# Two states in one scan tile: a selective scan in layer 1 regrouped as 64 channels x 2 states

## Chip, core and metric

The kernel runs on one core of a Trainium2 chip. The metric is the device time of one execution in microseconds (us). The core has five engines with a queue each: TensorE (PE in the profile, PEld for its weight loads), VectorE (DVE), ScalarE (ACT), GpSimd (POOL) and SyncE (SP, which issues most of the DMAs). SBUF is the working memory of 128 partitions, PSUM the memory that TensorE writes its sums to.

## The reference, cut to what matters

The program is a chain of four layers on images of 64 channels and 64 x 64 pixels. Only layer 1 is changed. It scans each image's 4096 pixels in four orders ("ways": by rows, by columns, and both backwards), with 128 channels and 16 states:

```
xs = concatenate([x_hwwh, flip(x_hwwh)], axis=1)        # 4 ways
x_dbl = einsum('bkdl,kcd->bkcl', xs, x_proj_w)
dts, Bs, Cs = split(x_dbl, [DT_RANK, DT_RANK + N], axis=2)
delta = softplus(einsum('bkrl,kdr->bkdl', dts, dt_w) + dt_b)
A = -exp(A_logs)

def step(h, inp):
    u, d, b, c = inp
    dA = exp(d[..., None] * A)
    h = dA * h + d[..., None] * b[:, :, None, :] * u[..., None]
    y = sum(h * c[:, :, None, :], axis=-1)
    return (h, y)
...
out_y = ys + xs * Ds
y = out_y[0] + inv_y[0] + unwh(out_y[1]) + unwh(inv_y[1])
```

So for each image, way, channel and state there is a first-order recurrence along 4096 pixels; its result is multiplied by C and summed over the 16 states, and the four ways are added up. What follows (normalization, gate, projection, feed-forward) is not changed.

## The kernel before

**Units of work.** An image's 4096 pixels are four chunks of T = 1024. One step (class `Step` in `layer1`) is one image b, one way k, one chunk j: 8 x 4 x 4 = 128 steps, in the order of line 1294's list, ways in the order 1, 3, 2, 0. A step has 16 scan tiles, one for each state, of 128 channels by 1024 pixels. `stream` (from line 433) runs through all 2048 tiles in one loop, software-pipelined by hand: the order of the instructions in this loop is the order in each engine's queue.

**One tile i, before.** Loads on SP (line 1239): one row of B and one of C, each broadcast from HBM to 128 partitions (512 KB each). `fetch(i + 5)` and `fetch_c(i + 3)` issue them ahead, into pools of four B tiles and five C tiles. `multiply_b(i + 2)` (line 484): GpSimd makes hb = du * B, into a pool of three. `decay(i + 2)` (line 491): ScalarE makes dA = exp(dt * A) in PSUM, two buffers. `scan(i)` (line 500): VectorE runs the recurrence over dA and hb; the result goes over dA in PSUM, or, for the states in `shared`, to an SBUF tile h. `multiply_c` (line 514): the product with C, on VectorE, or for the shared states 1, 4, 7, 10, 13 on GpSimd. ScalarE keeps the last column for the next chunk (`keep`, line 1249). `gather(i - 2)` calls `mm` (line 306): TensorE adds the product tile to the sum acc in PSUM with an identity matrix as weights; each 128x512 fp32 matmul stands as two passes in the profile, so a tile has four. When the last tile of a step is summed, `drain` (lines 1264 and 1266) moves acc to the image y: ScalarE copies it for the first way, VectorE adds it to y for the three others. `late` and `first` in the loop put a gather behind the background work or behind the scan.

**Preparing a step.** While a step runs, `prepare` makes the next one's data, one piece a tile from tile 2 on: TensorE projects u (x_dbl), ScalarE copies it and sends B and C to HBM, TensorE and ScalarE make dt (softplus), GpSimd makes du = dt * u (line 1236). dt and du are 128 channels by 1024 pixels, in two buffers each.

**Background tasks.** Preparing the images (`begin`), and normalization, output and feed-forward of those that are scanned (`finish`, `feed`), are cut into pieces that `advance` puts between the tiles, at one place in the loop. They use all engines and SP's queue (for instance line 910 loads 64-partition pieces of an image, lines 1133 and 1144 are VectorE's gating products, line 973 spreads a row over 128 partitions). A piece that holds the one PSUM buffer "mm" must be followed by its next ones before others come.

`Choice` is a pool that can be switched to a second one: while no scan runs, or at the end, the background tasks borrow the scan's tiles "dA" and "h".

Of the kernel before, what the change touches and what calls it, by code (L numbers as in the profile page):

```python
# [10 lines left out]
F32 = mybir.dt.float32  # L11
AF = mybir.ActivationFunctionType
ALU = mybir.AluOpType
# [93 lines left out]
def layouts(i):  # L107
# [29 lines left out]
    o["l1_dtb"] = i[p + "dt_b"].T  # L137
    o["l1_A"] = i[p + "A_logs"].reshape(4, 128, NS).transpose(1, 0, 2)
    o["l1_D"] = i[p + "Ds"].reshape(4, 128).T
# [68 lines left out]
def like(ap, ref):  # L208

    if len(ref.shape) == 2:  # L210
        return ap
    return ap.rearrange("p (a b) -> p a b", b=ref.shape[2])
# [38 lines left out]
class Choice:  # L251
# [5 lines left out]
    def tile(self, shape, dtype, name):  # L257
        if self.turns:
            self.second = not self.second
        return self.other.tile(shape, dtype, name=self.name) if self.second else self.pool.tile(shape, dtype, name=name)  # L260


def two(pool):


    return Ring([pool(f"pe{j}", 1, space=PSUM) for j in range(2)])


class Net:
# [313 lines left out]


    def layer0(self, src, dst):

# [272 lines left out]
    def layer1(self, src, dst):  # L859
        nc, tc, d = self.nc, self.tc, self.d  # L860
        mid = self.hbm["x1a"]
        with ExitStack() as ctx:
            pool = lambda n, b, **k: ctx.enter_context(tc.tile_pool(name="l1" + n, bufs=b, **k))
            cp, p1, p2, img, tp = pool("c", 1), pool("p1", 1), pool("p2", 2), pool("img", 2), pool("t", 5)
            pp = pool("pp", 1, space=PSUM)
            bp = pool("b", 4), pool("cc", 5)
            pools = (bp, pool("hb", 3), pool("hc", 3), pool("h", 3), two(pool), pool("pa", 1, space=PSUM))

            pp, tp = Choice(pp, pools[4], "dA"), Choice(tp, pools[3], "h")
            hp, h1 = pool("h3", 3, space=DRAM), pool("h1", 4, space=DRAM)  # L870
# [105 lines left out]
            def begin(b):  # L976
# [3 lines left out]
                ahead = {0: tokens(src, b, 0)}  # L980
                yield False

# [220 lines left out]
            class Step:  # L1203
                start, early, late = 2, 8, True
                shared = (1, 4, 7, 10, 13)
                shaped = staticmethod(lambda t: t)

                def __init__(self, b, k, j):
                    self.b, self.k, self.j, self.c, self.rev = b, k, j, 3 - j if k >= 2 else j, k >= 2
                    self.lanes = [(slice(None), A[:, k, :])]  # L1210

# [4 lines left out]
                def prepare(self):  # L1216
# [14 lines left out]
                    yield CALM  # L1231
                    dt = self.dt = p2.tile([128, T], F32, name="dt")
                    net.softplus_act(dt, pt, dtb[:, k : k + 1])
                    yield False
                    du = self.du = p2.tile([128, T], F32, name="du")
                    nc.gpsimd.tensor_tensor(like(du, u), like(dt, u), u, ALU.mult)

                def load(self, n, m, t):
                    nc.sync.dma_start(t, self.bc[m * NS + n : m * NS + n + 1, :].to_broadcast([128, T]))

# [11 lines left out]

                def skip(self, acc):
                    if self.k == 0:
                        net.mm(acc, skip[:, 0, :], self.u, start=True, stop=False)
                    return self.k == 0

                def drain(self, acc):
                    hold = images[self.b]
                    if self.k == ways[0] and self.j == 0:  # L1260
                        hold["y"] = img.tile([128, L], F32, name="img")
                    y = view(hold["y"], self.k, self.c)
                    if self.k == ways[0]:
                        nc.scalar.copy(y, like(acc, y))
                    else:
                        nc.vector.tensor_tensor(y, like(acc, y), y, ALU.add)  # L1266

# [16 lines left out]
            with tc.manual_schedule():  # L1284
# [9 lines left out]
                steps = [Step(b, k, j) for b in range(NB) for k in ways for j in range(4)]  # L1294
                self.stream(pools, (5, 2, 3), steps, behind, rest)

# [853 lines left out]
```

## Time and profile before

| what | value |
|---|---|
| three runs | 24767.98, 24765.61, 24763.93 us; median 24765.61 |
| profiled execution: span | 24763.3 us; the page lists no other time of its own beside it |
| layer 1's scan loop, first scan to last product | 1216 to 8487 us |
| its steady part, 2000 to 8000 us: VectorE, GpSimd, TensorE, ScalarE busy | 5471.63, 5562.17, 5165.06, 3262.36 us |
| the same: DMA share, GB/s | 0.90, 316 |
| products with B on GpSimd in it (line 484) | 1679 |
| loads of B and of C in it | 1678 and 1678, 512 KB each |
| products with C on VectorE and on GpSimd in it | 1153 and 524 |

How to read it: busy time is the time in which an engine executes, not the time in which it is held by another. A row of a group is: line, engine, operation, output<-inputs, shapes, count, then busy time, mean duration in ns, and the idle time before these instructions with what ended it. A row of waits is: who waited, for whom, us in total, how often, the longest. A row of the timeline is: start, duration (both us), engine, line, operation, tiles. A row of busy time by stretches has the stretch, its length, busy time and count for each engine, the clock granted to TensorE, the DMA share and the GB/s. Durations of neighbours overlap a little, so the distance from start to start is what an instruction costs in a dense queue.

### The profile page before, as it was taken

To read this page: it belongs to the slowest core of one execution; us is meant where nothing else is said; L and a number is where in the kernel's file an instruction comes from. 1 tells how busy PE (TensorE), PEld (TensorE's weight loads), DVE (VectorE), ACT (ScalarE), POOL (GpSimd) and SP (SyncE) were. 2 spreads that over 40 slices of the span, in tenths; PEclk is the share of its full clock that TensorE was granted. 3 is DMA by queue.
4 is the path that set the end of the run, shared out by engine and by line. 5 is a ranking of instruction groups with operands and counts; after the bars stand their busy time and mean duration, and the time that the engine had idled before them with its cause. 6 is when DMAs were issued, how large, how long until landed. Compare 5 with 4: busy or idle time off the path is not lost. (4 is left out here: it accounts for less than half of the span.)

```text
span 24763.3 us, 192937 instructions
## 1 busy us (share of the span) xinstructions
PE 21205.6 (86%) x53146; PEld 8272.3 (33%) x53146; DVE 22452.5 (91%) x12956; ACT 14796.2 (60%) x18824; POOL 22125.0 (89%) x10580
## 2 busy tenths in 40 slices
PE   8877888888888888888888888888888888888888
PEld 6522333333333323322333333333333333333333
DVE  5399999999999779978999999999999999999999
ACT  4355555555555456624666666666666666666666
POOL 0199999999999669977999999999999999999999
PEclk9888999999999999999999999999999999999999
DMA  2399899898998669933555555555555555555554
GB/s 65 93 319 326 308 321 318 310 319 314 313 318 311 238 211 339 343 103 93 168 173 169 173 167 173 168 173 167 173 169 173 168 173 169 173 169 173 169 173 158
DMA packets 1835292, 5282.68 MB, mean 213 GB/s; under 512 B 533712, under 2 KB 539924, under 8 KB 1831904
## 3 DMA queue, kind: packets, MB, share of 16 engines
q1 hardware_dynamic: 1809632, 5207.00, 63.0%
q10 hardware_dynamic: 24576, 63.33, 0.7%
q8 instruction: 423, 6.93, 0.1%
q14 instruction: 661, 5.41, 0.1%
HBM read 5112.85 MB, written 156.11 MB: 213 GB/s over the span
## 5 line engine op out<-in xcount | busy, mean ns | idle before, releaser
L484 POOL TENSOR_TENSOR hb<-du,bc 128x1024 f32<-128x1024 f32 x4608 | 10746.4, 2360 | 204.5 <-DVE h L500 137.9
L306 PE MATMUL acc<-hc,ident 128*128 128x512 f32 x18560 | 8788.0, 614 | 87.6 <-DVE img L1266 49.9
L491 ACT ACTIVATE dA<-dt,w_A 128x512 f32<-128x512 f32 x8192 | 5673.1, 693 | 3923.3 <-DVE hc L514 2873.1
L500 DVE TENSOR_TENSOR_SCAN dA<-dA,hb 128x1024 f32<-128x1024 f32 x3320 | 7580.9, 2283 | 188.4 <-ACT dA L491 101.0
L306 PE MATMUL acc<-h,ident 128*128 128x512 f32 x8064 | 4652.9, 706 | 2430.0 <-POOL h L514 2400.9
L306 PEld LDWEIGHTS acc<-hc,ident 128*128 128x128 f32 x18560 | 3639.8, 200 | 5214.2 <-issue 4562.5
L484 POOL TENSOR_TENSOR hb<-du,b 128x1024 f32<-128x1024 f32 x2048 | 4919.7, 2476 | 467.4 <-DVE dA L500 205.6
L514 DVE TENSOR_TENSOR hc<-dA,bc 128x1024 f32<-128x1024 f32 x3232 | 3956.8, 1224 | 244.4 <-issue 4.5
L491 ACT ACTIVATE dA<-dt,w_l_A 128x1024 f32<-128x1024 f32 x2560 | 2863.6, 1119 | 1004.6 <-DVE hc L514 764.6
L500 DVE TENSOR_TENSOR_SCAN h<-dA,hb 128x1024 f32<-128x1024 f32 x1416 | 3229.1, 2280 | 82.0 <-ACT dA L491 80.2
L306 PEld LDWEIGHTS acc<-h,ident 128*128 128x128 f32 x8064 | 1569.1, 212 | 5155.8 <-POOL h L514 3484.1
L514 POOL TENSOR_TENSOR h<-h,bc 128x1024 f32<-128x1024 f32 x1376 | 3243.1, 2357 | 8.3 <-DVE h L500 8.3
L500 DVE TENSOR_TENSOR_SCAN dA<-dA,carry,hb 128x1024 f32<-128x1024 f32 x1320 | 3094.2, 2344 | 124.9 <-POOL hb L484 57.2
L514 DVE TENSOR_TENSOR hc<-dA,c 128x1024 f32<-128x1024 f32 x1408 | 1723.7, 1224 | 118.3 <-DMA c<-bc 7.2
L514 POOL TENSOR_TENSOR h<-h,c 128x1024 f32<-128x1024 f32 x640 | 1566.4, 2447 | 7.5 <-ACT carry L1249 6.9
L491 ACT ACT_TABLE_LOAD x1128 | 1447.2, 1283 | 19.7
L500 DVE TENSOR_TENSOR_SCAN h<-dA,carry,hb 128x1024 f32<-128x1024 f32 x600 | 1404.6, 2341 | 36.4 <-ACT dA L491 25.2
L1249 ACT COPY carry<-dA 128x1 f32<-128x1 f32 x1056 | 169.4, 160 | 1654.3 <-DVE hc L514 1613.4
L2004 PE MATMUL mm<-xn,taps 128*128 128x512 f32 x2048 | 932.9, 597 | 1.1 <-ACT z L2052 1.1
L721 POOL MEMSET xf<- 128x24 f32 x33 | 4.3, 141 | 851.4 <-PE ps L742 725.2
L2019 PE MATMUL mm<-u,w_xp 128*36 128x512 f32 x1024 | 489.8, 601 | 143.0 <-ACT u L2016 136.3
L2039 POOL TENSOR_TENSOR du<-dt,u 128x1024 f32<-128x1024 f32 x256 | 603.0, 2355 | 9.9 <-ACT dt L415 9.9
(320 smaller groups left out, 18494.0 us busy)
## 6 DMA issues: line engine op xcount, KB each, us to landing
bc<-bc SPq DMA_DIRECT2D x4096, 512.0 KB
b<-bc SPq DMA_DIRECT2D x2048, 512.0 KB
c<-bc SPq DMA_DIRECT2D x2048, 512.0 KB
bc<-bc SPq DMA_DIRECT2D x512, 1024.0 KB
tmp<-rs SPq DMA_DIRECT2D x93, 512.0 KB
raw<-x SPq DMA_DIRECT2D x64, 512.0 KB
inv<-rs SPq DMA_DIRECT2D x64, 512.0 KB
tmp<-x SPq DMA_DIRECT2D x192, 128.0 KB
```

The source lines that it names most:

```text
L306: self.nc.tensor.matmul(o, lhsT, r, start=start, stop=stop)
L484: nc.gpsimd.tensor_tensor(s.shaped(hb[i]), s.shaped(s.du), B.pop(i), ALU.mult)
L491: nc.scalar.activation(dA[i][:, cut], s.dt[:, cut], AF.Exp, scale=A[:, n : n + 1])
L500: nc.vector.tensor_tensor_scan(h[:, way], dA[i][:, way], hb.pop(i)[:, way], s.first(n), ALU.mult, ALU.add)
L514: engine.tensor_tensor(s.shaped(o), s.shaped(h), CC.pop(i), ALU.mult)
L721: nc.gpsimd.memset(x[:, :, HW:], 0.0)
L1249: nc.scalar.copy(self.carry[:, n : n + 1], h[:, last : last + 1])
L2004: nc.tensor.matmul(tokens(px[:, j * W : j * W + W]), w.taps[k][:, m, j * 128 : j * 128 + 128], xn[:, :, f : f + HW], start=m == 0, stop=m ...
L2019: nc.tensor.matmul(pd, w.xp[:, k, j, :], u[:, j * W : j * W + W], start=j == 0, stop=j == 1)
L2039: nc.gpsimd.tensor_tensor(du, dt, u, ALU.mult)
```

## The change

A scan tile now holds 64 channels of two states: partitions 0 to 63 are state 2p, partitions 64 to 127 state 2p + 1; two tiles, one for each half h of the 128 channels, make a pair p. A step still has 16 tiles, in 8 pairs.

- Loads: one B tile and one C tile for a pair, each by two DMAs of 64 partitions (256 KB each), so half the bytes. The pools hold two B and three C tiles.
- dt and du are needed with each half of the channels on both halves of the partitions: `twofold` makes them by four SBUF-to-SBUF DMAs each (256 KB each). dt is now in a single buffer; du is made in place in it once dt is copied.
- B product: one GpSimd instruction for a pair (128 x 2 x 1024, the same B for both halves), into a pool of four pairs.
- The scan of a shared state writes over hb; the product with C always goes into hb, so the pools hc and h are gone. Shared tiles are 1, 4, 7, 10, 13 in even chunks and 1, 4, 6, 9, 12, 14 in odd ones.
- Sums: once for a pair, in four matmuls: for each 512 pixels and each channel half r, 128 rows by 64 columns, weights `ident2[:, :64]` (two identities on top of each other, which add the two states), into the partitions of that half.
- y of the ways before is added into the same sum by an identity matmul at its start, so `drain` is a ScalarE copy for every way.

```diff
+    def stream_pairs(self, pools, steps, behind, rest):
...
+        def fetch(p, m, pool, into):
+            if 2 * p < total:
+                into[p] = pool.tile([128, T], F32, name="bc"[m])
+                steps[2 * p // NS].load(p % (NS // 2), m, into[p])
+
+        def multiply_b(p):
+            if 2 * p < total:
+                s = steps[2 * p // NS]
+                hb[p] = hbp.tile([128, 2, T], F32, name="hb")
+                b = B.pop(p).unsqueeze(1).to_broadcast([128, 2, T])
+                nc.gpsimd.tensor_tensor(hb[p], s.du, b, ALU.mult)
+
+        def decay(i):
+            if i < total:
+                s, h, n = steps[i // NS], i % 2, i % NS // 2
+                dA[i] = pe.tile([128, T], F32, name="dA")
+                nc.scalar.activation(dA[i], s.dt[:, h, :], AF.Exp, scale=s.A[:, h * 8 + n : h * 8 + n + 1])
+
+        def scan(i):
+            s, h, n = steps[i // NS], i % 2, i % NS
+            a, b = dA[i], hb[i // 2][:, h, :]
+            o = b if shared(i) else a
+            way = slice(None, None, -1) if s.rev else slice(None)
+            nc.vector.tensor_tensor_scan(o[:, way], a[:, way], b[:, way], s.first(n), ALU.mult, ALU.add)
...
+        def multiply_c(i):
+            s, o = steps[i // NS], dA.pop(i)
+            engine = nc.gpsimd if shared(i) else nc.vector
+            engine.tensor_tensor(hb[i // 2][:, i % 2, :], o, CC[i // 2], ALU.mult)
...
+        def gather(p):
+            at, n = divmod(p, NS // 2)
+            if n == 0:
+                if at:
+                    steps[at - 1].drain(acc.pop(at - 1))
+                    steps[at - 1].done()
+                acc[at] = pa.tile([128, T], F32, name="acc")
+                begun[at] = steps[at].skip(acc[at])
+            h = hb.pop(p)
+            del CC[p]
+            for f in (0, 512):
+                for r in range(2):
+                    nc.tensor.matmul(
+                        acc[at][r * C : r * C + C, f : f + 512],
+                        self.ident2[:, :C],
+                        h[:, r, f : f + 512],
+                        start=n == 0 and not begun[at],
+                        stop=n == NS // 2 - 1,
+                    )
...
+        for i in range(total + 2):
+            at, n = divmod(i, NS)
+            need(i + 6, "bc")
+            need(i + 3, "du")
+            need(i + 2, "dt")
+            if 0 < i <= total and shared(i - 1):
+                multiply_c(i - 1)
+            if i % 2:
+                fetch(i // 2 + 2, 1, cp, CC)
+                multiply_b(i // 2 + 2)
+            else:
+                fetch(i // 2 + 3, 0, bp, B)
+
+            sums = i > 1 and i % 2
+            first = sums and n == 3 and i > NS
+            late = sums and not first and (shared(i - 2) or shared(i - 3))
+            if sums and not late and not first:
+                gather(i // 2 - 1)
...
@@ layer1
-            bp = pool("b", 4), pool("cc", 5)
-            pools = (bp, pool("hb", 3), pool("hc", 3), pool("h", 3), two(pool), pool("pa", 1, space=PSUM))
-
-            pp, tp = Choice(pp, pools[4], "dA"), Choice(tp, pools[3], "h")
+            pools = (pool("b", 2), pool("cc", 3), pool("hb", 4), two(pool), pool("pa", 1, space=PSUM))
+
+            pp, tp = Choice(pp, pools[3], "dA"), Choice(tp, Halves(pools[2]), "hb")
...
+                    self.A = A[:, k, :]
+                    self.shared = (1, 4, 6, 9, 12, 14) if j % 2 else (1, 4, 7, 10, 13)
+
+                def twofold(self, t, name):
+                    both = p2.tile([128, 2, T], F32, name=name)
+                    for h in range(2):
+                        for r in range(2):
+                            nc.sync.dma_start(both[r * C : r * C + C, h, :], t[h * C : h * C + C, :])
+                    return both
...
-                    dt = self.dt = p2.tile([128, T], F32, name="dt")
+                    dt = p1.tile([128, T], F32, name="dt")
                     net.softplus_act(dt, pt, dtb[:, k : k + 1])
+                    self.free = True
                     yield False
-                    du = self.du = p2.tile([128, T], F32, name="du")
-                    nc.gpsimd.tensor_tensor(like(du, u), like(dt, u), u, ALU.mult)
-
-                def load(self, n, m, t):
-                    nc.sync.dma_start(t, self.bc[m * NS + n : m * NS + n + 1, :].to_broadcast([128, T]))
+                    self.dt = self.twofold(dt, "dts")
+                    yield False
+                    yield False
+                    nc.gpsimd.tensor_tensor(like(dt, u), like(dt, u), u, ALU.mult)
+                    yield False
+                    self.du = self.twofold(dt, "dus")
+
+                def load(self, p, m, t):
+                    for r in range(2):
+                        row = m * NS + 2 * p + r
+                        nc.sync.dma_start(t[r * C : r * C + C, :], self.bc[row : row + 1, :].to_broadcast([C, T]))
...
                 def skip(self, acc):
+                    if self.k == ways[0]:
+                        return False
+                    net.mm(acc, net.ident, view(images[self.b]["y"], self.k, self.c), start=True, stop=False)
                     if self.k == 0:
-                        net.mm(acc, skip[:, 0, :], self.u, start=True, stop=False)
-                    return self.k == 0
+                        net.mm(acc, skip[:, 0, :], self.u, start=False, stop=False)
+                    return True
...
-                    if self.k == ways[0]:
-                        nc.scalar.copy(y, like(acc, y))
-                    else:
-                        nc.vector.tensor_tensor(y, like(acc, y), y, ALU.add)
+                    nc.scalar.copy(y, like(acc, y))
```

## The prediction

> **What bounds the kernel now.** I read first the busy time by stretches, to find layer 1 and what fills it; then the waits of VectorE and GpSimd there; then groups by shape, for prices; then VectorE's timeline, for the spacing of its instructions. The scan loop of layer 1 (lines 484 to 514 in the services of layer 1) runs from 1216 to 8487 us: 7271 us for 8 images x 4 ways x 4 chunks = 128 steps of 16 states, 56.8 us a step. Nothing outside layer 1 changes, so the prediction is a sum over these 128 steps. My steady window is 2000 to 8000 us: 1679 products on GpSimd (hb), so 104.9 steps of 57.2 us. The busy time by stretches:
> ```profile
> core 0: us, PE busy (x) PEld busy (x) DVE busy (x) ACT busy (x) POOL busy (x), PEclk, DMA share, GB/s
> 8943.20:8944.70 1.50, 0.00 (x0) 0.00 (x0) 0.00 (x0) 0.00 (x0) 0.00 (x0) 0.50 1.00 219
> ...
> 9600.00:9610.00 10.00, 9.35 (x21) 3.63 (x20) 9.93 (x7) 5.54 (x8) 10.00 (x5) 1.00 1.00 375
> 2000.00:8000.00 6000.00, 5165.06 (x11756) 1944.42 (x11755) 5471.63 (x3057) 3262.36 (x4047) 5562.17 (x2436) 0.93 0.90 316
> ```
> In the last line VectorE is busy 91%, GpSimd 93%, the DMA engines 90%, TensorE 86%: four near their limit. The other two lines are for later. What VectorE waits for in that window:
> ```profile
> DVE dA L500 <- ACT dA L491: 84.7, 64, 2.4
> DVE tmp L1133 <- PE mm L925: 68.1, 26, 6.6
> DVE tmp L1144 <- ACT tmp L1141: 64.3, 12, 5.4
> DVE dA L500 <- POOL hb L484: 57.4, 69, 1.8
> ```
> and GpSimd:
> ```profile
> POOL hb L484 <- DVE dA L500: 188.8, 94, 5.4
> POOL hb L484 <- DVE h L500: 135.9, 123, 3.0
> POOL hb L484 <- DMA b<-bc: 54.4, 55, 4.3
> ```
> The reader is to see who holds whom: GpSimd waits 325 us for VectorE to free an hb buffer, VectorE only 57 for a product. So VectorE sets the pace, and adds about 4.2 us a step (440 us over 104.9 steps) of small waits, most for the background tasks (image preparation, feed-forward), whose results come late from TensorE or ScalarE. VectorE's own spacing:
> ```profile
> 4019.88 2.35 DVE L500 TENSOR_TENSOR_SCAN dA<-dA,carry,hb 128x1024 f32<-128x1024 f32 x1
> 4022.32 1.23 DVE L514 TENSOR_TENSOR hc<-dA,c 128x1024 f32<-128x1024 f32 x1
> 4023.46 2.34 DVE L500 TENSOR_TENSOR_SCAN h<-dA,carry,hb 128x1024 f32<-128x1024 f32 x1
> 4025.72 2.33 DVE L500 TENSOR_TENSOR_SCAN dA<-dA,carry,hb 128x1024 f32<-128x1024 f32 x1
> ```
> A state whose C product VectorE makes costs 2.44 + 1.14 = 3.57 us from start to start, a shared one (product on GpSimd) 2.26. One step: 11 x 3.57 + 5 x 2.26 = 50.6, drains (line 1266, three steps of four, about 1.4 net) 1.05, other work 1.7 (about 150 instructions of some 1.2 us over 104.9 steps): 53.3, and 3.9 of waits. GpSimd: its products start 2.33 us apart where they are dense (start times in the trace); 16 x 2.33 + 5 x 2.31 + du 2.5 + other 1.0 = 52.4.
>
> **What the Trainium skill says.** GPSIMD Engine Reference, § 3.1: a two-input product of 2048 fp32 takes 4497 ns. This trace has no such width; its slope agrees (below). TensorEngine Tiling (Array Packing), § Theoretical Speedup: an output of at most 64 columns lets two tiles work at once, up to 2x. The trace agrees (0.231 against 0.51 us a pass, below). SBUF — State Buffer, § Door 1: a transfer to 64 partitions reaches 8 of the 16 ports, 196 GB/s against 328, and two transfers to the two halves serialize. The first two lines of the stretches fit: at 8943 us only 64-partition loads of 257 KB run (x<-hx, line 1585), and full DMA engines move 219 GB/s; at 9600 us 128-partition broadcasts move 375. The same page, § Who interferes with whom: VectorE with one SBUF input doesn't hold GpSimd up. Scan and C product keep one SBUF input each (the other is PSUM), so I price no new conflict.
>
> **The change, part by part, per step.**
> *B product of two tiles.* 16 instructions of 1024 elements become 8 of 2048. The widths that the trace has:
> ```profile
> L484 POOL TENSOR_TENSOR hb<-du,b 128x1024 f32<-128x1024 f32 x2048 | 4919.7, 2476 | 467.4 <-DVE dA L500 205.6 <-DVE h L500 166.9 <-DMA b<-bc 60.8
> ...
> L855 POOL TENSOR_TENSOR x<-x,g 128x512 f32<-128x512 f32 x32 | 40.7, 1273 | 99.3 <-DVE g L854 98.8 <-DVE w_l_D L880 0.4
> ```
> Undelayed, 1024 take 2.36 (layers 2 and 3), 512 take 1.27: 1.09 per 512, so 2048 take 4.54, or 4.5 apart. Bounds 4.43 (slope from the 560-wide form) and 4.66 (two old ones). Taken 4.5: 8 x (4.66 - 4.5) = 1.3 us less. That B is repeated over the two tiles costs nothing: layer 3 repeats it so at 2.36.
> *Shared states 5 to 5.5* (6 in odd chunks): GpSimd + 0.5 x 2.31 = 1.15; VectorE - 0.5 x 1.31 = 0.65.
> *y in the sum.* VectorE loses the drain, 1.05. ScalarE gains three drains of four: 1.91 (strided, line 1264) or about 1.05: 1.0 a step on an engine 54% busy. Behind it in ScalarE's queue stand a carry copy and the exp of the second next tile, for which VectorE waits; that exp's buffer is freed by VectorE only 3.5 us later, so 0, at worst 1.4, at best 0: the copy adds work and frees nothing sooner. TensorE gains two matmuls (2 us).
> *Sums in column halves.* 64 passes a step either way. Now (2227 + 1205) us / 6712 = 0.51 each, 32.7 us; with 64 output columns:
> ```profile
> L376 PE MATMUL pc<-strip,vin 128*64 128x512 f32 x384 | 88.8, 599 | 1.3 <-ACT g L1410 1.3
> ```
> 88.8 / 384 = 0.231, so 15 us. TensorE falls from 49 to about 34 us. It isn't the bound; what counts is that background matmuls come sooner (the 68 us above).
> *VectorE after:* 53.3 - 0.65 - 1.05 = 51.6. *GpSimd after:* 52.4 - 1.3 + 1.15 = 52.3 (51.7 to 53.6). The bound passes to GpSimd, 1 us under the old one.
> *DMA.* B and C fall from 32 x 512 KB = 16.8 MB to 8.4, dt and du doubled add 2.1 MB, the rest stays at 1.3. But all the new ones write 64 partitions: at 219 GB/s 10.5 MB take 48 us, with the rest 52 of 55; at 375 it would be 32. SP issues 40 instead of 32 at about 0.35 us: no bound.
> *New waits.* (a) B has two buffers of two states, so its load goes out when the product two before is done and must land within one product and one or two C products, 7.1 us; a landing is about 2 us of latency (a load of line 910 issued at 1136.8 moves its first packet at 1138.1, and the end has to be reported) and 2.4 of transfer at 219 GB/s, plus what is queued ahead. Before, loads ran five states ahead. On SP, behind a waiting B stand C (three buffers, not urgent) and background loads. (b) du is made in place in dt: on GpSimd it waits until the four copies of dt have landed, about 7 us after their issue, two states earlier; the next B product is queued behind it. (c) the copies of du must land before the next step's first B product, again about 7 us in odd chunks. On SP they wait for softplus and for du, with B loads queued behind. I put (a) to (c) at 0.9 us a step, from 0 to 7. (d) hb is freed by TensorE's sum and no longer by the scan, but there are eight tiles of it and not three, so GpSimd's 3.1 us a step of waiting for VectorE should shrink to about 1. With 1.0 of its other waits, which I leave:
>
> 52.3 + 0.9 + 1.0 + 1.0 = 55.2 us a step, 2.0 less than 57.2. Times 128: 256 us. The profiled execution spans 24763.3 us (the page gives no other time of its own; the median of the runs is 24765.6, 2.3 more, under 0.02%). 24763 - 256 = 24507, rounded **24510 us**.
>
> **Rivals.** *The waits go too:* with TensorE at 60% and deep hb buffers GpSimd might run nearly without gaps, as it does in layer 2 (98% busy at 9000 to 10500 us). 52.3 / 0.98 = 53.3 a step: 3.9 x 128 = 500 less, 24263. Against it: background tasks still break in. *Nothing gained:* GpSimd's load is the same as before (52.3 against 52.4); if a product of two tiles costs 4.66, or its long block delays C products so that TensorE and behind it the background tasks wait longer, the step stays at 57: 24740. That column halves don't overlap, the change not doing what it says, ends here too. *Slower, by late B loads:* with 64-partition writes at 219 GB/s the queue stays 94% full although half the bytes are gone, and two blocks of 1 MB (4.8 us each) stand ahead of B loads that have 7.1 us. If each block costs GpSimd some 2.5 us and the single loads 1.4 more, 52.3 + 6.4 = 58.7: +1.5 x 128 = 192, 24955. It decides once a B load takes over 7 us to land. For it: the 219 GB/s; against it: loads of 128 KB to alternating halves (line 910) ran at full packet speed when isolated (84 ns for 2 KB).
>
> **Chances.** Forecast 0.42 (24350 to 24650), waits gone 0.22, nothing gained 0.13, slower 0.23. A measurement of this kernel can tell about 0.2% (50 us) from no change: faster 0.64, same 0.13, slower 0.23. The range runs from 24230, below the case of the waits gone, to 24900, most of the way to the slower case; beyond its ends I leave 0.05 and 0.12. Both signs are in it; the forecast's own range stands above.
>
> **What would show it.** Products hb at 4.5 us; sums at 0.23 to 0.28 us a pass and TensorE near 60%; no VectorE drain; GB/s in layer 1 near 190, with a DMA share near 0.9 if 64-partition writes are slow, near 0.6 if not; GpSimd above 94% busy, with "POOL hb <- DMA b" below 100 us over 6000. I am wrong if that last wait grows to several hundred, if VectorE waits for hb by hundreds, or if du on GpSimd waits for dt's copies by more than 2 us each.

## The result, and the profile after

The changed kernel takes 25294.4 us (median of 4 runs, 25289.4 to 25307.6) against 24764.8 (24762.3 to 24768.0) for the kernel before: a ratio of 1.0215, interval 1.0201 to 1.0230. It is slower by 530 us, where 255 us less was forecast, and lies beyond the upper end of the forecast's range, 24900. The profiled execution took 25289.4 us, its span is 25287.6. The scan loop of layer 1, from its first scan to its last product, now runs from 1239 to 9005 us, 7766 us. Counted in the same way the kernel before took 7267 (its first scan stands at 1220). So about 500 of the 530 us lie in the loop, 3.9 us for each of the 128 steps; the first scan starts 18 us later, and what follows the loop takes 6 us longer.

Busy time by stretches, kernel after, the window shown of before:

```profile
core 0: us, PE busy (x) PEld busy (x) DVE busy (x) ACT busy (x) POOL busy (x), PEclk, DMA share, GB/s
2000.00:8000.00 6000.00, 4211.07 (x11262) 1220.47 (x11259) 4976.94 (x2743) 3134.72 (x3864) 5217.17 (x1546) 0.81 0.79 192
```

Before, four columns of this line stood near their limit. Now none does: VectorE 83%, GpSimd 87%, TensorE 70%, DMA share 0.79. The work has shrunk, and idle time has more than filled the room. The window holds 787 pair products (group below), 8 for a step, so 98.4 steps of 61.0 us.

Groups of instructions, kernel after (count, then busy us and mean ns, then idle time before and what ended it):

```profile
L621 POOL TENSOR_TENSOR hb<-dus,b 128x2048 f32<-128x2048 f32 x787 | 3624.0, 4619 | 402.2 <-PE acc L665 137.5 <-issue 78.7 <-DMA dus<-dt 77.9
L1390 POOL TENSOR_TENSOR dt<-dt,u 128x1024 f32<-128x1024 f32 x98 | 255.3, 2605 | 221.4 <-DMA dts<-dt 209.3 <-DMA c<-bc 6.9 <-ACT dA L627 2.7
```

The prices on GpSimd were right to within 3%: a pair product was put at 4.5 us and takes 4.62. GpSimd's work is 5217 / 98.4 = 53.0 us a step (forecast 52.3). Its idle time is 783 / 98.4 = 8.0 us a step, where the sum had 2.9. What it waits for:

```profile
POOL dt L1390 <- DMA dts<-dt: 209.3, 91, 4.5
POOL hb L621 <- PE acc L665: 137.5, 58, 5.6
POOL hb L621 <- issue: 78.7, 27, 9.7
POOL hb L621 <- DMA dus<-dt: 77.9, 18, 9.5
POOL hb L649 <- ACT carry L1407: 75.2, 39, 6.5
POOL hb L621 <- DMA b<-bc: 72.5, 41, 4.8
```

Before, the first two rows of GpSimd's waits named VectorE. Now no row shown does (its products with C wait 26.0 us for VectorE): GpSimd waits for DMAs (dts, dus, b: 360 us) and for pair buffers. A pair buffer is set free by TensorE's sum; the row with "PE acc" says so, and the row "issue" (time for which the profile names no cause) belongs to it too, since both go when there are more buffers (run e8). The waits of VectorE:

```profile
DVE dA L637 <- POOL hb L621: 367.0, 184, 7.7
DVE dA L637 <- ACT dA L627: 166.3, 90, 10.3
DVE tmp L1212 <- POOL tmp L1207: 107.8, 24, 6.9
DVE hb L637 <- POOL hb L621: 81.6, 32, 4.7
```

Two rows, 449 us, wait for a pair product: 57 before. GpSimd now sets the pace, and hands on its stops.

Where the stops come from is read from the timeline. ScalarE copies the finished sum of the step before to the image y, and later makes dt for the next step, which is ready at 4031.04 us:

```profile
4024.25 1.01 ACT L1424 COPY img<-acc 128x1024 f32<-128x1024 f32 x1 [0.38 <-ACT dbl L1374]
4029.92 1.12 ACT L426 ACTIVATE dt<-mm,w_l_dtb 128x1024 f32<-128x1024 f32 x1
```

SyncE's queue after that (start, duration, engine, line, operation, tiles):

```profile
4037.72 1.08 SPq L1397 DMA_DIRECT2D b<-bc  x2
4038.90 3.39 SPq L1360 DMA_DIRECT2D dts<-dt  x4
4042.39 1.96 SPq L1397 DMA_DIRECT2D c<-bc  x2
4044.45 1.18 SPq L1397 DMA_DIRECT2D b<-bc  x2
4045.73 1.18 SPq L1397 DMA_DIRECT2D c<-bc  x2
4049.47 3.06 SPq L1360 DMA_DIRECT2D dus<-dt  x4
```

and GpSimd's:

```profile
4027.67 2.35 POOL L649 TENSOR_TENSOR hb<-hb,c 128x1024 f32<-128x1024 f32 x1 [5.24 <-ACT carry L1407]
4033.11 9.13 POOL L621 TENSOR_TENSOR hb<-dus,b 128x2048 f32<-128x2048 f32 x2 [3.09 <-PE acc L665]
4042.20 2.36 POOL L649 TENSOR_TENSOR hb<-hb,c 128x1024 f32<-128x1024 f32 x1
4047.09 2.35 POOL L1390 TENSOR_TENSOR dt<-dt,u 128x1024 f32<-128x1024 f32 x1 [2.53 <-DMA dts<-dt]
4049.40 4.61 POOL L621 TENSOR_TENSOR hb<-dus,b 128x2048 f32<-128x2048 f32 x1
```

The copies of dt stand behind a load of B. That load needs the buffer which the product in progress reads (the first half of the 9.13 us, to 4037.7), so the copies of a finished dt wait 7.9 us for a product that has nothing to do with it. du starts at 4047.09, 16 us after dt is ready, the pair product queued behind it is 2.5 us late, and its copies go out at 4049.47 only. The second stop stands earlier: the product at 4033.11, the fifth of its step, waited 3.09 us for a pair buffer. With four buffers it takes over that of the step's first pair. TensorE at that time:

```profile
4025.93 3.45 PE L317 MATMUL acc<-img,ident 128*128 128x512 f32 x4
4029.21 1.88 PE L317 MATMUL acc<-u,skip 128*128 128x512 f32 x4
4031.02 3.65 PE L665 MATMUL acc<-hb,ident 128*64 128x512 f32 x16
```

TensorE was not idle. The first pair's products with C had ended at 4008.54 and 4017.84, but its sum had to wait for ScalarE's copy of the old sum (to 4025.26), then for the matmuls that put y into the new sum (4025.93 to 4029.38), then for those with the skip weights (to 4031.09; only the last way has them). The first pair is summed at 4032.96, and GpSimd's product starts 0.15 us later.

This is the rule and not a single case. Of the 216 us that GpSimd waits for pair buffers in the window ("PE acc" and "issue"), 185 stand at the fifth product of a step, and the run has its own control: in the 24 steps of the first way, whose sum does not begin with y, the fifth product waits 0.3 us in all; in the 74 steps of the other ways it waits 185 us (1.5 us each in the second way, 1.9 in the third, 3.9 in the fourth). Run e12, which takes y out of the sum, says the same. TensorE spends more on y than was thought:

```profile
L317 PE MATMUL acc<-img,ident 128*128 128x512 f32 x300 | 267.2, 1038 | 17.7 <-ACT carry L1407 15.1 <-ACT img L1424 2.4
```

Four of these make a step's y, so they take 3.6 us, where the forecast had 2. The sums themselves show 3.65 / 16 = 0.23 us a pass in the row above, as forecast.

### The profile page after: what moved, and what is told of

It is laid out like the page before. It is cut to its first block, busy times and chain, and to the rows that moved or that the text cites. A ratio compares the mean times of both kernels' runs of the same rounds, so it can differ in the third digit from the quotient of the medians.

```text
span 25287.6 us, 192014 instructions
## 1 busy us (share of the span) xinstructions
PE 20407.3 (81%) x53530; PEld 7490.1 (30%) x53530; DVE 22256.1 (88%) x12796; ACT 14895.1 (59%) x18920; POOL 22132.6 (88%) x9620
## 5 line engine op out<-in xcount | busy, mean ns | idle before, releaser
L317 PE MATMUL acc<-hc,ident 128*128 128x512 f32 x12928 | 6064.6, 612 | 6.6 <-DVE hc L525 6.6
L621 POOL TENSOR_TENSOR hb<-dus,b 128x2048 f32<-128x2048 f32 x1024 | 4716.3, 4621 | 514.5 <-PE acc L665 175.5
L317 PE MATMUL acc<-h,ident 128*128 128x512 f32 x5504 | 3173.7, 706 | 1773.1 <-POOL h L525 1749.8
L317 PEld LDWEIGHTS acc<-hc,ident 128*128 128x128 f32 x12928 | 2511.1, 198 | 3519.3 <-issue 3179.5
L665 PE MATMUL acc<-hb,ident 128*64 128x512 f32 x8192 | 2587.1, 732 | 985.4 <-POOL hb L649 968.4
L627 ACT ACTIVATE dA<-dts,w_l_A 128x1024 f32<-128x1024 f32 x2048 | 2285.7, 1117 | 861.4 <-DVE hb L649 549.0
L637 DVE TENSOR_TENSOR_SCAN dA<-dA,carry,hb 128x1024 f32<-128x1024 f32 x992 | 2326.2, 2345 | 414.7 <-POOL hb L621 250.8
L649 POOL TENSOR_TENSOR hb<-hb,c 128x1024 f32<-128x1024 f32 x704 | 1671.7, 2375 | 146.9 <-ACT carry L1407 103.5
L649 DVE TENSOR_TENSOR hb<-dA,c 128x1024 f32<-128x1024 f32 x1344 | 1646.2, 1225 | 155.5 <-DMA c<-bc 83.5
L637 DVE TENSOR_TENSOR_SCAN hb<-dA,carry,hb 128x1024 f32<-128x1024 f32 x544 | 1273.9, 2342 | 188.9 <-POOL hb L621 116.0
```

The costliest lines, as they stand in the source:

```text
L317: self.nc.tensor.matmul(o, lhsT, r, start=start, stop=stop)
L621: nc.gpsimd.tensor_tensor(hb[p], s.du, b, ALU.mult)
L627: nc.scalar.activation(dA[i], s.dt[:, h, :], AF.Exp, scale=s.A[:, h * 8 + n : h * 8 + n + 1])
L637: nc.vector.tensor_tensor_scan(o[:, way], a[:, way], b[:, way], s.first(n), ALU.mult, ALU.add)
L649: engine.tensor_tensor(hb[i // 2][:, i % 2, :], o, CC[i // 2], ALU.mult)
L665: nc.tensor.matmul(acc[at][r * C : r * C + C, f : f + 512], self.ident2[:, :C], h[:, r, f : f + 512], start=n == 0 and not begun[at], stop ...
```

## The experiments

**Theories.** Theory 1: the chain dt, copies, du, copies, and its place in SyncE's queue. Theory 2: transfers to 64 contiguous partitions use a part of the DMA engines, so everything lands late. Theory 3: GpSimd, TensorE and VectorE are coupled by four pair buffers and long products. Times are medians. The kernel before, measured again beside the versions, stood at 24757 to 24775 us, so a difference between two versions that were not measured together is uncertain by up to some 20 us. Sums of waits below are those of GpSimd in the same window, 2000 to 8000 us.

**e1: du in its own tile.**

```diff
-                    dbl = p1.tile([68, T], F32, name="dbl")
+                    du = p1.tile([128, T], F32, name="dbl")
+                    dbl = du[:68]
...
-                    nc.gpsimd.tensor_tensor(like(dt, u), like(dt, u), u, ALU.mult)
+                    nc.gpsimd.tensor_tensor(like(du, u), like(dt, u), u, ALU.mult)
...
-                    self.du = self.twofold(dt, "dus")
+                    self.du = self.twofold(du, "dus")
```

> du gets a tile of its own, so that its product need not wait until the four copies of dt have landed; nothing else changes. Theory 1 (the chain dt, copies, du, copies is what costs): GpSimd's wait of 209 us in 6000 (91 waits in 98.4 steps, 2.1 us a step) goes, and the time falls by about 2.1 x 128 = 270 us to 25020. Theory 2 (the 64-partition loads take too much of the DMA engines, so B, dt and du come late): the wait goes, another load is late next, within 60 us of 25294. Theory 3 (VectorE and GpSimd are coupled too tightly: long pair products, and an hb buffer that only TensorE's sum sets free): within 60 us of 25294, the wait turning up at another product.

Measured 25279.2: 15 us less, which is nothing by this measure. The 209 us wait is gone, and the waits for dus (78 to 148), B (73 to 157) and C (16 to 52) have grown by nearly as much. Theory 1, as a wait of du, falls. dt's copies still go out 7.8 us after dt is ready (mean over the window, as in the changed kernel), and du's follow them more closely: du starts 14.0 us after dt in place of 16.4. The loads of B behind these copies leave later for it: by the start times in the traces, the eight loads of a step leave 5.3 us in sum after the product that frees their buffer, against 3.9 in the changed kernel.

**e2: the copies of dt issued by ScalarE.**

```diff
-                def twofold(self, t, name):
+                def twofold(self, t, name, queue=nc.sync):
...
-                            nc.sync.dma_start(both[r * C : r * C + C, h, :], t[h * C : h * C + C, :])
+                            queue.dma_start(both[r * C : r * C + C, h, :], t[h * C : h * C + C, :])
...
-                    self.dt = self.twofold(dt, "dts")
+                    self.dt = self.twofold(dt, "dts", nc.scalar)
```

> The four copies of dt are issued by ScalarE right after softplus in place of SyncE, where they stand behind a load of B that waits for a product of GpSimd. Theory 1: the copies go out several us earlier, du's wait of 2.1 us a step goes and dus lands earlier: 25000 to 25100. Theory 2: the copies leave earlier but take as long; 25200 to 25300. Theory 3: within 60 us of 25294.

Measured 24996.8: 298 us less. The copies go out about 0.2 us after dt is ready, and GpSimd's waits for the DMAs of dts, dus, B and C fall from 376 to 138 us. What is left of them is mostly B, whose wait does not fall (72.5 before):

```profile
POOL hb L621 <- DMA b<-bc: 90.9, 61, 9.3
POOL hb L621 <- DMA dus<-dt: 30.7, 9, 8.1
```

du starts 14.5 us after dt, no earlier than in e1, so what costs is not that du waits, but when the copies leave and what they hold up. The run moves two things at once: the copies go earlier, and SyncE's queue is rid of them (3.4 us of issue in the timeline above), so that the loads of B leave 1.7 us a step late in place of 3.9. Which of the two is worth more was not separated.

**e3: whole loads of B and C.**

```diff
-                    for r in range(2):
-                        row = m * NS + 2 * p + r
-                        nc.sync.dma_start(t[r * C : r * C + C, :], self.bc[row : row + 1, :].to_broadcast([C, T]))
+                    row = m * NS + 2 * p
+                    nc.sync.dma_start(t, self.bc[row : row + 1, :].to_broadcast([128, T]))
```

> Each load of B and C is one DMA of 128 partitions in place of two of 64: both halves get the row of the even state, so B and C of the odd states are left out. Same bytes, half the DMA instructions[...]. Theory 2: B and C land early, the waits for DMA go (72 us for B and 67 us for C in 6000, and part of those for dt and du): 24700 to 24900. Theory 1: dt's copies still stand behind the loads that wait for GpSimd: 25200 to 25290. Theory 3: within 60 us of 25294.

Measured 25053.1: 241 us less, at DMA share 0.64 in place of 0.79. That is more than theory 1 allowed and less than theory 2 wanted. It doesn't say whether the half of the partitions or the number of DMAs did it.

**e4: no doubling.**

```diff
-                    self.dt = self.twofold(dt, "dts")
+                    self.dt = dt.unsqueeze(1).to_broadcast([128, 2, T])
...
-                    self.du = self.twofold(dt, "dus")
+                    self.du = du.unsqueeze(1).to_broadcast([128, 2, T])
```

(dt and du are in two buffers each, as in the kernel before.)

> No doubling of dt and du: the scans and products read dt and du themselves, repeated for both halves, so the exchange of channel halves between the partitions is left out, and with it eight DMAs a step on SyncE and all that waits for them. Theory 1: the whole loss goes: about 24780, the time of the kernel before, or below. Theory 2: some DMA traffic goes too, but B and C stay at 64 partitions: 25000 to 25150. Theory 3: above 25100.

Measured 24757.0: 537 us less, the time of the kernel before (ratio 0.9993, 0.9984 to 1.0001). Without the doubling the loss is gone, but nothing of the forecast gain is there: GpSimd still waits 188 us for pair buffers, 174 of them at the fifth product.

**e5: the two states on alternate partitions.** Partition 2c + r in place of 64 r + c, with A laid out to match, and the sums' weights made of pairs.

```diff
-                            nc.sync.dma_start(both[r * C : r * C + C, h, :], t[h * C : h * C + C, :])
+                            nc.sync.dma_start(both[r:128:2, h, :], t[h * C : h * C + C, :])
...
-                        nc.sync.dma_start(t[r * C : r * C + C, :], self.bc[row : row + 1, :].to_broadcast([C, T]))
+                        nc.sync.dma_start(t[r:128:2, :], self.bc[row : row + 1, :].to_broadcast([C, T]))
...
+            self.pairs = cp.tile([128, C], F32, name="pairs")
+            nc.vector.tensor_tensor(self.pairs, self.ident[:, 0:128:2], self.ident[:, 1:128:2], ALU.add)
```

> The two states lie on alternate partitions (partition 2c + r in place of 64r + c): every DMA of B, C, dt and du still has 64 partitions and there are as many of them, but each is spread over all partitions in place of one half. Theory 2a (a half of the partitions is served by a part of the DMA engines, and that is what made whole loads 241 us faster): at most 25053, with a lower DMA share than 0.79, and nearer 24950 since the copies gain too. Theory 2b (it was the number of DMA instructions on SyncE): within 60 us of 25294.

Measured 25071.0: 223 us less, nearly e3's gain (18 us short of what theory 2a asked for at least) with as many DMAs as before. Busy time by stretches, this run:

```profile
2000.00:8000.00 6000.00, 4279.15 (x11591) 1235.62 (x11590) 5114.89 (x2820) 3221.68 (x3972) 5331.45 (x1589) 0.82 0.62 198
```

A DMA share of 0.62 at 198 GB/s, against 0.79 at 192: the same bytes take a quarter less of the engines' time. The number of instructions (theory 2b) is not it.

**e6: no doubling and whole loads** (e3's and e4's edits together).

> No doubling of dt and du, and whole loads of B and C, together (leaves out what those two leave out). If the two costs are independent, 537 and 241 us add: 24515, which is the step of 55.2 us of the forecast. If whole loads were faster only because dt's copies stood behind shorter loads, there is nothing more to gain: 24700 to 24757.

Measured 24710.3, 47 us under e4 (33 if each is held against the kernel before measured beside it), where 241 would have meant an independent cost: the half-partition transfers cost little but through dt and du.

**e7: alternate partitions, and dt's copies on ScalarE** (e2's and e5's edits together).

> Alternate partitions, and the copies of dt issued by ScalarE. If place in the queue (298 us) and rate of the transfers are independent costs, about 24755 or less, the time of the kernel before. If they are one cost (the moment at which dt and du have landed), 24900 to 25000.

Measured 24823.0 (ratio 1.0026, 1.0015 to 1.0037). 298 + 223 = 521 us were to be had if the costs add, and 471 came: place in the queue and rate of the transfer are nearly separate costs. GpSimd's waits for dts, dus, B and C are down from 376 to some 70 us.

**e8: no doubling, six pair buffers.**

```diff
-            pools = (pool("b", 2), pool("cc", 3), pool("hb", 4), two(pool), pool("pa", 1, space=PSUM))
+            pools = (pool("b", 2), pool("cc", 3), pool("hb", 6), two(pool), pool("pa", 1, space=PSUM))
```

> No doubling of dt and du (which leaves out the exchange of channel halves), and six pair buffers in place of four in the room that this frees. Theory 3 (a pair buffer that only TensorE's sum sets free holds GpSimd up: 123 us for the sum and 65 us of issue in 6000 without the doubling, 1.9 us a step): 24757 falls by up to 240, to about 24520. If GpSimd's own work bounds the step, less than 60 us.

Measured 24544.7 (ratio 0.9913, 0.9898 to 0.9928): 212 us under e4. GpSimd's waits in this run:

```profile
POOL hb L649 <- ACT carry L1408: 151.5, 72, 7.5
POOL hb L649 <- DVE hb L637: 67.8, 22, 7.3
POOL tmp L1207 <- DMA tmp<-hz: 36.4, 13, 5.0
...
POOL hb L621 <- PE acc L665: 3.1, 2, 2.8
```

The wait for TensorE's sum falls from 123 us in e4 to 3, and that of "issue" from 65 to nothing. Theory 3 holds for the buffers. GpSimd is 95% busy, and the step is as long as the forecast's 55.2: 55.3 us (868 pair products).

**e9: alternate partitions, dt on ScalarE, five pair buffers.** The room is one tile for dbl, dt and du, and two buffers of C.

```diff
-            pools = (pool("b", 2), pool("cc", 3), pool("hb", 4), two(pool), pool("pa", 1, space=PSUM))
+            pools = (pool("b", 2), pool("cc", 2), pool("hb", 5), two(pool), pool("pa", 1, space=PSUM))
...
-                fetch(i // 2 + 2, 1, cp, CC)
+                fetch(i // 2 + 1, 1, cp, CC)
```

> The run with alternate partitions and dt's copies on ScalarE (24823), with five pair buffers in place of four. The room comes from one tile for x_proj's copy, dt and du, and from two buffers of C in place of three, each loaded one pair later. If a pair buffer freed only by TensorE's sum still holds GpSimd up (141 us for the sum and 66 us of issue in 6000 there), about 24823 minus most of the 212 us that two more buffers gave without the doubling: 24620 to 24680, below the kernel before. Rival: C, loaded later, comes too late for VectorE's product, and the time stays at 24823 or rises, with the wait for C above 100 us in 6000.

Measured 25064.7: the rival of the expectation. VectorE's first wait in this run:

```profile
DVE hb L649 <- DMA c<-bc: 489.7, 218, 12.4
```

The products no longer wait for a pair buffer (2.5 us of "issue" are left, and no "PE acc" row), but C comes too late, and that costs more.

**e10: the same, with a shared state's last column copied by VectorE.**

```diff
-                        nc.scalar.copy(self.carry[:, n : n + 1], h[:, last : last + 1])
+                        put = nc.vector.tensor_copy if n in self.shared else nc.scalar.copy
+                        put(self.carry[:, n : n + 1], h[:, last : last + 1])
```

> The run before this one, with the copy of a shared state's last column made by VectorE right after its scan in place of ScalarE. GpSimd's C product, which writes over that column, then no longer waits for ScalarE (97 us in 6000, 0.9 us a step). If GpSimd sets the pace, about 60 to 100 us below the run before this one; if VectorE does, up to 60 us above it (5.5 small copies a step).

Measured 25040.5, 24 us less, between the two cases. C's delay decides in both runs, so this tells little about the copy.

**e11: the pair product in two instructions.**

```diff
-                nc.gpsimd.tensor_tensor(hb[p], s.du, b, ALU.mult)
+                for h in range(2):
+                    nc.gpsimd.tensor_tensor(hb[p][:, h, :], s.du[:, h, :], b, ALU.mult)
```

> The changed kernel with the B product made in two instructions of 1024 columns in place of one of 2048, into the same pair buffer. By the forecast the pair product saves 1.3 us a step on GpSimd: 25294 + 160 = 25455. By the measured 4.62 us a pair against 2.33 a single one it saves 0.3: 25294 + 40. Rival (the long product makes VectorE wait for both halves when it needs the first, 2.3 us, twice a step): 24900 to 25200.

Measured 25239.5: 55 us less. Neither of the two prices foresaw a gain, and it is short of the rival's 24900 to 25200. Two products take 2 x 2385 = 4770 ns in place of 4619, so a step has 8 x 0.15 = 1.2 us more work on GpSimd (the forecast said 1.3) and is yet shorter. VectorE can begin with the first half, and its wait for the product falls from 449 to 161 us, and part of that turns up as a wait for C (67 to 237).

**e12: y added by VectorE again.**

```diff
-                    if self.k == ways[0]:
-                        return False
-                    net.mm(acc, net.ident, view(images[self.b]["y"], self.k, self.c), start=True, stop=False)
                     if self.k == 0:
-                        net.mm(acc, skip[:, 0, :], self.u, start=False, stop=False)
-                    return True
+                        net.mm(acc, skip[:, 0, :], self.u, start=True, stop=False)
+                    return self.k == 0
...
-                    nc.scalar.copy(y, like(acc, y))
+                    if self.k == ways[0]:
+                        nc.scalar.copy(y, like(acc, y))
+                    else:
+                        nc.vector.tensor_tensor(y, like(acc, y), y, ALU.add)
```

> The changed kernel with y added by VectorE at a step's end in three steps of four, as before the change, in place of y in the same sum and a copy by ScalarE. By the forecast this gives VectorE 1.05 us a step back: if VectorE sets the step, 25294 + 134 = 25430. If GpSimd and its waits set it, within 50 us of 25294. If the copy by ScalarE or y's matmul ahead of the first sum held the pair buffers, 25150 to 25240.

Measured 25197.0: 97 us less, although VectorE has more to do. GpSimd's wait for pair buffers ("PE acc" and "issue") falls from 216 to 124 us, and that of the fifth product from 185 to 48: the third case expected. Of these 48, 36 stand in the last way, whose sum still begins with the skip matmuls.

**e13 and e14: e7 with y added by VectorE, without and with the split product.**

> Alternate partitions, dt's copies on ScalarE, and y added by VectorE at a step's end again. If the costs add, 24823 - 97 = about 24725, just below the kernel before. If VectorE, no longer held up by dt and du, is what sets the pace there, its 1.05 us a step come back: 24850 to 24960.

> The run before this one with the pair product in two instructions. If the 55 us that this gave the changed kernel add too: about 24670. If they came only from VectorE's waits while du was late: 24725 to 24780, GpSimd having 0.3 us a step more to do.

Measured 24762.0 and 24790.0. e13 is 61 us under e7, where 97 would have meant that the costs add, and equal to the kernel before (ratio 0.9996, 0.9987 to 1.0004). The split product now costs 28 us in place of saving 55, a little more than its second case had. That GpSimd's added work counts once dt and du are in time fits this.

**e15: six pair buffers without the doubling, y added by VectorE.**

> No doubling of dt and du (which leaves out the exchange of channel halves), six pair buffers, and y added by VectorE again. If y in the sum costs only by holding the pair buffers until a later first sum, that cost is gone with six: 24545 to 24680. If it costs in itself (ScalarE's copy ahead of an exp, y's matmul on TensorE): about 24450.

Measured 24597.2, 52 us above e8 (some 34 if each is held against the kernel before measured beside it). With four buffers y in the sum cost 97 us (61 in e13, with the copies mostly in time), with six it saves some: its cost came through the pair buffers. With six buffers the fifth product waits 3 us in all (e8) or not at all (e15).

**e16: the kernel before, with y in the sum alone** (e12's edit the other way).

> The kernel before with this part of the change alone: y goes into the same sum, and ScalarE copies it out in every step. By the forecast VectorE loses 1.05 us a step: 24770 - 134 = 24636. If y's matmul or the copy delays the first sum and the kernel's buffers wait for it, 24770 to 24870.

Measured 24738.9 (ratio 0.9986, 0.9979 to 0.9992): 36 us less, a quarter of the 134 expected, in a kernel where a product's buffer is freed by the scan.

**e17 and e18: five pair buffers, the room taken from du.** e7 with one buffer for du's doubled tile, its copies issued after the last product of the step before; e18 with three buffers of B besides (dbl, dt and du share one tile to make the room).

```diff
-                    both = p2.tile([128, 2, T], F32, name=name)
+                    both = (p1 if name == "dus" else p2).tile([128, 2, T], F32, name=name)
...
+                    while not hasattr(self, "go"):
+                        yield False
                     self.du = self.twofold(dt, "dus")
```

(`go` is set once the last product of the step before is issued.)

> Alternate partitions, dt's copies on ScalarE (24823), five pair buffers in place of four; the room comes from one buffer for du's doubled tile in place of two, filled after the last product of the step before. If the pair buffers hold GpSimd up here too: 24620 to 24700, below the kernel before. Rival: du's copies, which may start only two states before they are needed, land too late (about 4 us of DMA in 7 us), and GpSimd waits for dus: 24823 or above.

> The run before this one, with three buffers of B in place of two (dbl, dt and du share one tile to make the room), so that a load of B on SyncE waits for an earlier product of GpSimd and du's copies and C's loads behind it leave sooner. If SyncE's order still costs: 50 to 100 us below the run before this one; if not, within 30 us of it.

Measured 25235.8 and 25151.6: the rival again; the third buffer of B gives 84 us back. SyncE's waits in e17:

```profile
SPq L1404 <- POOL hb L621: 2346.2, 640, 8.1
SPq L1365 <- POOL hb L621: 514.5, 98, 9.2
```

The second row is new: du's copies stand 5 us a step in SyncE's queue until the old tile is read, with B's loads behind them, and GpSimd then waits 301 us for B and 147 for dus; for the sum it waits 5.4. Of the versions that compute the whole reference none beats the kernel before but e16, by 0.14%.

## Why the prediction was wrong

**The engines' work on GpSimd and in the sums: right.** GpSimd 52.3 forecast, 53.0 measured (52.7 in e8: 5716 busy us in 108.5 steps); the pair product 4.5 against 4.57 to 4.62, near the 4497 ns that the Trainium skill gives (GPSIMD Engine Reference, § 3.1); sums 0.23 us a pass where dense; 192 GB/s against 190. The bound did pass to GpSimd. The product with C on GpSimd takes 2.37 us (2.44 before), so no new conflict with VectorE shows.

**The failed step: "I put (a) to (c) at 0.9 us a step, from 0 to 7".** What hangs on the doubling, (b) and (c), is worth 4.2 us a step by itself (e4: 537 / 128). The step's range held that; the value chosen did not. The working looked at how long each transfer takes. What it missed stands in the order of SyncE's queue: it said that the loads of B wait behind the copies, and did not see that the copies themselves wait behind a load of B, which waits for a product on GpSimd. The copies left 7.8 us after dt was ready; with that gone (e2) 2.3 us a step came back, and with the transfers spread over all partitions (e5) 1.7. The two are nearly separate (e7), and together they are most of the 4.2. SyncE's own work was priced too low as well: 0.35 us for a DMA, where a load takes 0.55 to 0.61 and a copy 0.68 to 0.86 (means of the window), 24.6 us a step for 40 of them in place of 14.

**Step (d): "GpSimd's 3.1 us a step of waiting for VectorE should shrink to about 1" failed in kind.** It compared eight tiles with three, and not what a tile is held for. Before, an hb buffer was freed by the scan; now a pair buffer stays from the product until the sum, past scan, C product and everything ahead of the sum in TensorE's queue. "PE acc" and "issue" stand at 216 / 98.4 = 2.2 us a step, and two more buffers were worth 212 / 128 = 1.7 (e8 against e4). That is why e4, with no copies at all, only reaches the time of before.

**y in the sum: put at no cost, failed.** The forecast asked of the copy on ScalarE only whether it delays an exp ("so 0"), and of y's matmuls only how long they take. It did not ask what stands behind them: the first sum of a step, which frees the buffer that the fifth product needs. That is where 185 of the 216 us of step (d) arise, in the ways with y alone. Undone in the changed kernel, y in the sum gives 97 us, 0.76 a step (e12). Its gain, 1.05 us a step on VectorE, no longer counted where GpSimd sets the pace; with six buffers y in the sum is worth up to 52 us (e15), alone in the kernel before 36 (e16).

**The sum again.** 55.2 was 52.3 of work and 2.9 of waits. Measured: 53.0 + 8.0 = 61.0. Missing were 0.7 of work and 5.1 of waits, 5.8 x 128 = 742 of the 784 us between forecast and result. Of the rest, some 25 us lie outside the loop. Of what the forecast said would show it, TensorE came out 70% busy (near 60 was said), GpSimd 87% (above 94), and the DMA share 0.79, between the 0.9 of slow and the 0.6 of fast transfers.

**The rivals.** "Slower, by late B loads" had the sign and named the transfers (24955, a third of the loss). Its mechanism was not the one: B itself was late by 72.5 us in 6000, under the 100 set as a sign, and the 64-partition rate cost 223 us, almost all through dt and du (e6: 47 without them). That loads of B leave late did come true, but through the copies ahead of them in the queue (3.9 us a step in sum, 0.5 in e4). The Trainium skill's statement on the ports (SBUF — State Buffer, § Door 1) was thus to the point, and e5 agrees with it: spreading the same 64 rows over all partitions brings the DMA share from 0.79 to 0.62. That transfers to the two halves serialize is said a section further on in that page ("Can I just issue two DMAs to hit both halves?"); no run here tests it alone. Two of the signs named for being wrong came true: VectorE waits 449 us for hb, and du waits 2.3 us each (209.3 in 91) for dt's copies. The latter was the right place and the wrong cause: with du's wait gone (e1), nothing was gained.

**What stays open.** Whether six pair buffers would help as much with the doubling in place: both ways of making room for a fifth (e9, e17) brought another wait in its stead. Why e1 gains nothing was read from the moments of issue and the waits that grew, and not tried by itself; nor was it tried whether e2 gains by the earlier copies or by the freer queue. That y ahead of the first sum holds the pair buffers is shown by the ways and by e12, but e4 was not run without y in the sum.

## What to carry to other kernels

Before pricing a new DMA, write down what stands ahead of it in its queue and what that waits for: a transfer that is ready can stand 8 us behind a load that needs a buffer from an unrelated product. Count buffers by who frees them: four pair buffers freed at the end of the chain were scarcer here than three tiles freed in its middle. Then look at what stands ahead of the instruction that frees a buffer: a few matmuls before a step's first sum were cheap for TensorE, which had time, and held up GpSimd. A wait that the profile names may be removed and nothing gained; move the event that comes late instead.

## What was not expected of the hardware

A DMA to 64 alternate partitions (every second one) is not the same as one to 64 contiguous ones: 0.62 of the DMA engines' time at 198 GB/s against 0.79 at 192, and 223 us of the kernel. Two 1024-column products on GpSimd in place of one of 2048 cost 0.15 us more (4.77 against 4.62). The clock granted to TensorE was lower where TensorE was less busy in the window: 0.93 at 5165 us busy (before), 0.81 at 4211 (after), 0.80 at 4127 (e12); what that does to the end was not tried.
